# Twenty-nine of a graph kernel's gathers are replaced by row-by-row DMAs from ScalarE and SyncE

## The chip, the cores and the metric

One core of one Trainium2 chip. The core has five engines, each with its own in-order instruction stream: TensorE (PE; its weight loads are listed apart as PEld), VectorE (DVE), ScalarE (ACT), GpSimd (POOL) and SyncE (SP). They meet only at semaphores. DMAs are issued by ACT, SP and POOL and run beside the engines. The metric is device microseconds for one run of the kernel; less is better.

## The reference

One graph attention layer on 12,500 nodes of 128 features and 200,000 edges sorted by target node:

```python
edge_index = jnp.stack([src, dst])
h = jnp.maximum(_layernorm(x, axis=-1), 0.0)
x = x + _L0_gnn_ref(h, edge_index, edge_attr_64, W_node, W_edge, a)

# _L0_gnn_ref, 4 heads of 32 features:
h = (node_features @ W_node.T).reshape(num_nodes, H, HD)
e = (edge_features @ W_edge.T).reshape(num_edges, H, HD)
h_src = h[src]
h_tgt = h[tgt]
att = jnp.sum(jnp.concatenate([h_src, h_tgt, e], axis=-1) * a, axis=-1)
att = jnp.where(att > 0, att, 0.2 * att)
m = jnp.maximum(segment_max(att, tgt), 0.0)
ex = jnp.exp(att - m[tgt])
denom = segment_sum(ex, tgt) + (num_edges - deg)[:, None] * jnp.exp(-m)
w = ex / denom[tgt]
h_prime = segment_sum(w[:, :, None] * h_src, tgt)
```

So for each edge the row of its source node has to be fetched, weighed by a softmax over all edges of the same target, and added up at the target.

## The kernel before

A first part computes for every node one row of 137 floats (548 bytes): the 128 projected features with a one behind each head, a count, and the node's share of the attention for each head. The rows go to a table in DRAM (`table`), and all that follows works on edges.

The edges are cut into 392 groups of up to 511 (with one carried place, 512, stored as J = 4 chunks of 128). QG = 4 groups are a **quad** (98 quads), and up to four quads are a **superblock**; from quad 7 to 86 superblocks have four quads each, beginning at 7, 11, 15 and so on. Up to quad 35 a quad has one window of target nodes, up to 74 two, from 75 on four (`CLASSES`).

*Gathers.* `gather` (L171) has POOL issue one indirect DMA for each chunk (L183): it takes 128 places from `srci` and brings 128 rows into `ga`, one on each partition. `ga_all` is a ring of QUADS = 8 quads. `open_logits(q)` (L644) calls `fetch(q + 2)`, which issues quad q + 2's sixteen gathers. From quad 8 on, every gather adds to one semaphore for each ring place, and the reader waits for the sum.

*Logits.* `all_logits(q)` (L1368) runs ahead of the softmax: DVE compares targets (L656), PE multiplies edge features (L686) and adds the targets' share (L689), and ACT copies the result (`keep_logits`, tg, L699). `add_sources(q)` (L718) has ACT wait for all gathers of quad q and then copy the sources' attention out of `ga` into U (L733). It is called at the beginning of `all_logits(q + 1)`, behind that quad's first DVE comparison, or at the start of `softmax` for a superblock's last quad.

*Softmax.* `softmax(s)` (L769) works on a whole superblock once the U of its last quad is there: PE turns U (L790), ACT and DVE alternate (L795 to L872), PE turns the result back (L882), ACT copies it to xs (L888).

*Sums.* `sums(q)` (L1054) goes through the four groups of a quad, one **step** each: DVE weighs the gathered rows (L1041 or L1082) and builds the selection (L1024 or L1084), PE multiplies the two into the accumulator (L1115, four chunks, two records each), and in between `passed_on` (L934) has ACT compute an exponential (L943) and DVE pass a row on (L949). `complete(new)` ends a step, and `issue("inputs", "results")` follows. The sums of a superblock run beside the logits of the next.

*SP's queue.* SP issues, in the order written by `issue` (L592), results, input rows, edge features, targets and window weights (L596). For addresses that are known only at run time it first loads them from SBUF into registers (`windows`, L582; a TENSOR_LOAD in the trace).

The order of all this is written out by hand (`tc.manual_schedule()`): `together` runs the generators of logits, sums and softmax in turn, one yield each, and each engine executes its instructions in the order in which this emits them.

The targets' buffer `db_all` has room for two quads of 32-bit places. From quad OFFSETS = 10 on targets are bytes and use its first quarter only.

Of the kernel before, what the change touches and what calls it, by code (L numbers as in the profile page):

```python
# [9 lines left out]
F32 = mybir.dt.float32  # L10
# [4 lines left out]
OP = mybir.AluOpType  # L15
AX = mybir.AxisListType

P = 128
# [28 lines left out]
SQUARE = 32  # L47
TWO = 2
HELD = 3
SETS = max(NODE_T, QG * J)  # L50
PAD = 1 << 20

# [5 lines left out]
def class_of(q):  # L58

    return next(c[1:] for c in CLASSES if c[0] is None or q < c[0])  # L60
# [9 lines left out]
def kernel(  # L70
# [39 lines left out]
    nc = tc.nc  # L110
    NT = -(-(N + P) // P)
    NP = NT * P
# [8 lines left out]
    table = dram.tile([NP, ROW], F32, name="table")  # L121
# [33 lines left out]
    quads = blocks(G, QG)  # L155
    nq = len(quads)
# [7 lines left out]

    spare = consts.tile([P, 6 * SBG * H], F32, name="spare")
    ga_all = consts.tile([P, QUADS, QG, J, ROW], F32, name="ga")
    GA, GATHERED = {}, set()
    arrived = [tc.alloc_semaphore(f"rows{k}") for k in range(QUADS)]
    landings = {}

    def gather(q, rows, width, lo, hi):  # L171

        g0, m = quads[q]
        ga = GA[q] = ga_all[:, q % QUADS]
        chunks = lambda i: -(-min(E - (g0 + i) * NE + 1, GE) // P)
        for i in range(lo, hi):
            if chunks(i) < J:
                nc.vector.memset(ga[:, i, chunks(i):, :], 0.0)
        order = [(i, j) for i in range(lo, hi) for j in range(chunks(i))]
        if q >= 2 * QUADS:  # L180
            order.sort(key=lambda at: at != (hi - 1, 0))
        for i, j in order:
            came = nc.gpsimd.indirect_dma_start(  # L183
                out=ga[:, i, j, 0:width], out_offset=None, in_=rows,
                in_offset=bass.IndirectOffsetOnAxis(ap=srci[:, g0 + i, j:j + 1], axis=0))
# [16 lines left out]
    per = SBG // QG  # L202
# [15 lines left out]
    with tc.manual_schedule():  # L218
# [25 lines left out]
        for _ in range(AT_ONCE):  # L244
            q, i = early.pop(0)
# [129 lines left out]
        db_all = stay.tile([P, 2, QG, GE], I32, name="db")  # L375
# [20 lines left out]
        with tc.tile_pool(name="node", bufs=2) as node, tc.tile_pool(  # L396
# [6 lines left out]
            first = index.tile([1, W], F32, name="first")  # L403
# [110 lines left out]
            for b, (t0, T) in enumerate(sets):  # L514
# [5 lines left out]
                row = node.tile([P, NODE_T, ROW], F32, name="row")  # L520
# [24 lines left out]
    with tc.tile_pool(name="work", bufs=2) as work, \  # L545
# [34 lines left out]
        def windows(of, size, w, n):  # L580
# [52 lines left out]
        def fetch_rows(s):  # L633
            g0, m = groups(s)
            dr = DR[s] = turned.tile([SBG * H, NE + 2], I32, name="dr", bufs=2)
            if finer(s) > 1:
# [4 lines left out]
            nc.sync.dma_start(dr[0:H * m, :],  # L641
                              dst_rows[g0:g0 + m, :].unsqueeze(0).to_broadcast([H, m, NE + 2]))

        def open_logits(q):  # L644
            if q == supers[of_quad[q]][0]:
                fetch_rows(of_quad[q])
            if q + 2 < nq:
                fetch(q + 2)
            AT[q] = work.tile([P, QG, GE], BF16, name="at")
# [68 lines left out]
        def add_sources(q):  # L718

            s = of_quad[q]  # L720
            g0, m = quads[q]
            s0, sm = groups(s)
            keep_logits(q)
            if s not in U:
                U[s] = turned.tile([P, J, SBG * H], F32, name="U", bufs=2)
            f = finer(s)
            u = U[s][:, 0:J // f, 0:sm * H * f].rearrange("p c (h w) -> p w c h", h=H)[
                :, (g0 - s0) * f:(g0 - s0 + m) * f]
            if q >= QUADS:
# [3 lines left out]
            taken = nc.scalar.copy(u, GA[q][:, :m].rearrange("p g (f c) r -> p (g f) c r", f=f)[  # L733
                :, :, :, R_SRC:R_SRC + H])
# [160 lines left out]
        state = {"step": 0}  # L895

        def complete(window=True, all_due=False):

            state["step"] += 1
            division = None  # L900
            if divisions and "hold" not in state and (
                    all_due or divisions[0][-1] is None or divisions[0][-1] + 2 <= state["step"]):
                division = divisions.pop(0)
            if begun and window:
                complete_window(*begun.pop())
            if division:
                divide(*division)
# [146 lines left out]
        def sums(q):  # L1054
# [7 lines left out]
            g0, m = quads[q]  # L1062
            s = of_quad[q]
# [3 lines left out]
            k, span = class_of(q)  # L1067
# [23 lines left out]
            for i in range(m):  # L1091
                g = g0 + i
                if first_fold - 4 <= q < first_fold - 4 + FOLDS:
                    shifts(q + 4, i)
                on_gpsimd = early and (q, i) > (first_fold - 2, QG - 2)
                if (q, i) not in AHEAD:
                    weighed(nc.gpsimd if on_gpsimd else nc.vector, ga, i,
                            heads(XE[s] if on_gpsimd else ex)[:, :, :, g - s0])
                    if not early:
                        mark(q, i, hot)  # L1100
                new = i % k == 0
                if not i and not later:
                    entered()
                    settled()
                if new:
                    second = k == 2 and i > 0
                    if not second:
                        bank = ps.tile([P, 512], F32, name="acc", bufs=3)
                    acc = bank[0:1 + span, ROW:2 * ROW] if second else bank[0:1 + span, 0:ROW]
                    fc = fac if g == s0 else None  # L1110
                if later and i == m - 1:
                    entered()
                least_j = 1 if k == 1 else 0
                for j in range(least_j, J)[::-1]:
                    nc.tensor.matmul(acc, hot[:, i, j, 0:1 + span], ga[:, i, j, :],  # L1115
                                     start=new and j == J - 1 and not second,
                                     stop=k > 1 and i % k == k - 1 and j == least_j,
                                     skip_group_check=k > 1)
                if i == (2 if later else 1):
                    passed_on(fac if g0 == s0 else None)  # L1120
                    if later:
                        settled()
                if not later and i == (2 if k > 1 else 1):
                    entered()
                    if k == 1:
                        settled()
                complete(new)
                if k == 1:
                    begun.append((q, i, ga, hot, pt, acc, fc))
                if i == 2 and QUADS <= q < first_fold - 5 and of_quad[q + 1] == s:  # L1130
# [715 lines left out]
```

## Time and profile before

| | before |
|---|---|
| median of 3 runs | 1998.38 us (1997.35 to 1998.41) |
| the profiled execution: time, span | 1998.91 us, 1997.1 us |
| POOL busy | 1496.7 us (75%), 1596 instructions |
| DVE busy | 1195.0 us (60%) |
| PE busy | 1130.1 us (57%), mean granted clock 0.734 |
| ACT busy | 318.9 us (16%) |
| gathers from `table` (L183) | 1494, 946 ns mean |

A line of the groups reads: line, engine, operation, out<-in, shapes, count; then busy time and the mean of one in ns; then the engine's idle time just before them and what ended most of it. A line of the timeline reads: start and duration in us, engine, line, operation, out<-in, shapes, count; in brackets the engine's idle time before it and what ended it. SPq and ACTq are the sequencers of SP and ACT: DMA issues and register loads, which are not counted as busy. A line of one source line's view reads: line, engine, operation, count; durations min/median/max in ns; first and last start in us.

### The profile page before, as it was taken

To read this page: it belongs to the slowest core of one execution; us is meant where nothing else is said; L and a number is where in the kernel's file an instruction comes from. 1 tells how busy PE (TensorE), PEld (TensorE's weight loads), DVE (VectorE), ACT (ScalarE), POOL (GpSimd) and SP (SyncE) were. 2 spreads that over 40 slices of the span, in tenths; PEclk is the share of its full clock that TensorE was granted. 3 is DMA by queue.
4 is the path that set the end of the run, shared out by engine and by line. 5 is a ranking of instruction groups with operands and counts; after the bars stand their busy time and mean duration, and the time that the engine had idled before them with its cause. 6 is when DMAs were issued, how large, how long until landed. Compare 5 with 4: busy or idle time off the path is not lost.

```text
span 1997.1 us, 18760 instructions
## 1 busy us (share of the span) xinstructions
PE 1130.1 (57%) x5116; PEld 771.6 (39%) x5116; DVE 1195.0 (60%) x2666; ACT 318.9 (16%) x1077; POOL 1496.7 (75%) x1596
## 2 busy tenths in 40 slices
PE   6566675555464645554646455546464555365555
PEld 4444454334243333343434333434343333243344
DVE  8676886456374554563755546637555475376675
ACT  6564111001001010010010100101101011121222
POOL 7777777777777777777777777777777777777775
PEclk9788788676676776766767767667677677677777
DMA  7753754434344434344444444444443453444441
GB/s 253 208 138 95 179 131 114 99 98 109 98 110 102 119 98 106 104 109 111 113 105 121 98 112 107 110 111 112 107 117 94 106 123 97 110 108 115 106 102 43
DMA packets 167747, 229.56 MB, mean 115 GB/s; under 512 B 60827, under 2 KB 100669, under 8 KB 167638
## 3 DMA queue, kind: packets, MB, share of 16 engines
q0 software_dynamic: 50112, 109.61, 24.5%
q1 hardware_dynamic: 115824, 116.14, 20.1%
q10 hardware_dynamic: 1702, 2.59, 0.4%
q8 instruction: 41, 0.67, 0.1%
q14 instruction: 68, 0.56, 0.1%
HBM read 210.74 MB, written 17.43 MB: 114 GB/s over the span
## 4 chain that ended last, share of the span: by engine, by line
POOL 41%; DVE 24%; issue 16%; PE 7%; DMA 6%; ACT 5%; SPq 0%; ACTq 0%; POOLq 0%; DVEq 0%
POOL ga L183 41%; DMA ga<-table,srci 5%; DVE at L656 3%; PE t_ps L790 2%; DVE ga L1041 1%; DVE t_ps L865 1%; DVE t_ps L804 1%; DVE t_ps L803 1%; DVE t_ps L862 1%; PE ex_ps L882 1%; DVE hot L1024 1%; PE acc L1115 1%; DVE stats L287 1%; ACT ga L309 1%; DVE pt L949 1%
## 5 line engine op out<-in xcount | busy, mean ns | idle before, releaser
L183 POOL DMA_INDIRECT ga<-table,srci x1494 | 1413.4, 946 | 456.7 <-issue 429.4
L1115 PE MATMUL acc<-ga,hot 128*113 128x137 f32 (+1 forms) x2928 | 539.4, 343 | 77.7 <-DVE hot L1024 53.3
L1115 PEld LDWEIGHTS acc<-ga,hot 128*113 128x113 f32 (+1 forms) x2928 | 479.9, 213 | 176.6 <-issue 94.5
L949 DVE SCALAR_TENSOR_TENSOR pt<-pt,spare,acc 1x133 f32<-1x133 f32 x113 | 38.2, 338 | 522.0 <-ACT den_of L943 520.6
L689 PE MATMUL lg<-at,pw 112*96 112x512 bf16 (+2 forms) x392 | 155.5, 433 | 278.1 <-DVE at L656 265.4
L686 PE MATMUL lg<-ea,by_pair 128*96 128x512 f32 (+1 forms) x392 | 227.8, 666 | 6.4 <-ACT tg L699 6.4
L656 DVE TENSOR_TENSOR at<-const_ps,db 112x1024 bf16<-112x1024 f32 (+1 forms) x176 | 212.9, 1210 | 4.5 <-DMA db<-offset 4.5
L1082 DVE TENSOR_TENSOR ga<-ga,ex_ps 128x1056 f32<-128x1056 f32 x147 | 182.2, 1240 | 0.0
L790 PE MATMUL t_ps<-ident,U 128*64 128x128 f32 (+2 forms) x210 | 46.8, 395 | 217.5 <-ACT U L733 217.5
L733 ACT COPY U<-ga 128x64 f32<-128x64 f32 x98 | 29.0, 297 | 815.8 <-DMA ga<-table,srci 815.8
L1084 DVE TENSOR_TENSOR hot<-const_ps,slot 128x896 f32<-128x896 f32 (+1 forms) x147 | 144.2, 981 | 0.0
L790 PEld LDWEIGHTS t_ps<-ident,U 128*64 128x64 f32 (+2 forms) x210 | 36.8, 200 | 243.8 <-ACT U L733 240.1
L882 PE MATMUL ex_ps<-ident,stack 128*128 128x128 f32 x105 | 28.6, 424 | 178.2 <-DVE stack L872 166.9
L968 PEld LDWEIGHTS acc<-pt,spare 1*2 1x2 f32 x226 | 14.0, 86 | 208.8 <-issue 199.9
L689 PEld LDWEIGHTS <-pw 112*96 112x96 bf16 (+2 forms) x392 | 53.9, 137 | 100.9 <-issue 98.4
L882 PEld LDWEIGHTS ex_ps<-ident,stack 128*128 128x128 f32 x105 | 18.5, 214 | 192.1 <-ACT stack L870 192.1
L183 POOL DMA_INDIRECT ga<-in_x_dram,srci x72 | 68.6, 952 | 23.2 <-issue 19.2
L1041 DVE TENSOR_TENSOR ga<-ga,ex_ps 128x528 f32<-128x528 f32 x92 | 63.6, 693 | 36.6 <-ACT xs L888 36.5
L699 ACT COPY tg<-lg 96x512 f32<-96x512 f32 (+1 forms) x51 | 29.5, 579 | 294.0 <-PE lg L689 294.0
L913 PE MATMUL acc<-ga,hot 128*81 128x137 f32 x176 | 42.6, 330 | 54.9 <-ACT ga L921 52.9
L715 PE MATMUL t_ps<-tg,of_head 96*64 96x512 f32 (+3 forms) x96 | 71.6, 838 | 0.0
L715 PEld LDWEIGHTS t_ps<-tg,of_head 96*64 96x64 f32 (+3 forms) x96 | 11.9, 172 | 153.8 <-issue 151.6
(204 smaller groups left out, 1324.9 us busy)
## 6 DMA issues: line engine op xcount, KB each, us to landing
ea<-in_edge_t_dram SPq DMA_DIRECT2D x196, 256.0 KB
ga<-table,srci POOLq DMA_INDIRECT x1494, 2.6
db<-offset SPq DMA_DIRECT2D x53, 256.0 KB
db<-in_dst_dram SPq DMA_DIRECT2D x20, 320.0 KB
db<-offset SPq DMA_DIRECT2D x35, 160.0 KB
table<-row SPq DMA_DIRECT2D x9, 616.5 KB
xt<-in_x_dram SPq DMA_DIRECT2D x9, 576.0 KB
inputs<-in_x_dram SPq DMA_DIRECT2D x92, 56.0 KB
```

The costliest lines, as they stand in the source:

```text
L183: came = nc.gpsimd.indirect_dma_start(out=ga[:, i, j, 0:width], out_offset=None, in_=rows, in_offset=bass.IndirectOffsetOnAxis(ap=srci[:, ...
L656: nc.vector.tensor_tensor(AT[q][:span, i:i + n, :].rearrange("p g e -> p (g e)"), part_ps[:span].to_broadcast([span, n * GE]), DB[q][:span ...
L686: nc.tensor.matmul(lg, by_pair[:, begin:begin + n], ea[:, i // 2, :], start=half == 0 and i == 0, stop=False, skip_group_check=True)
L689: nc.tensor.matmul(lg, PW[q][:span, begin:begin + n], at[:span, i, :], start=False, stop=full and i == quads[q][1] - 1, skip_group_check=True)
L715: nc.tensor.matmul(TP[s][:groups(s)[1] * H], of_head[supers[s][1], p][:n], tg[:n], start=p == 0, stop=False, skip_group_check=True)
L790: nc.tensor.matmul(t_ps[:R, j * P:(j + 1) * P], u[:, j, :R], ident, start=False, stop=j == C - 1, skip_group_check=True)
L882: nc.tensor.transpose(turned_ps[:, j, :], stack[:, j * P:(j + 1) * P], ident)
L949: nc.vector.scalar_tensor_tensor(to, row(w + at), passing[:, w + at:w + at + 1], own, op0=OP.mult, op1=OP.add)
L1041: engine.tensor_tensor(val, val, weight.unsqueeze(3).to_broadcast([P, J, H, HW]), op=OP.mult)
L1082: nc.vector.tensor_tensor(val, val, weight.unsqueeze(3).to_broadcast([P, TWO * J, H, HW]), op=OP.mult)
L1084: nc.vector.tensor_tensor(hot[:, i:i + TWO, :, 1:1 + span].rearrange("p g j c -> p (g j) c"), lane_ps[:, 0:span].unsqueeze(1).to_broadcast ...
L1115: nc.tensor.matmul(acc, hot[:, i, j, 0:1 + span], ga[:, i, j, :], start=new and j == J - 1 and not second, stop=k > 1 and i % k == k - 1 a ...
```

## The change

29 of the chunks, the fourth or third chunk of the last group of some quad, are no longer gathered by POOL. Each is brought as 128 DMAs of one row (548 bytes, one partition) each:

- **ACT's 16 chunks** (fourth chunk, j = 3), for quads 16, 20, 24 ... 76: one for each superblock of four quads that begins at quad 11, 15 ... 71, for the second quad of the next superblock. In `add_sources` of the superblock's four quads, ahead of the wait for gathers, ACT issues 12, 30, 54 and 32 of the rows (`IN_WAITS`).
- **SP's 13 chunks** (third chunk, j = 2), for quads 20, 24, 29 ... 77: from quad 10 on SP issues seven rows behind each step of the sums, so a chunk takes 19 steps.

The place of a row comes from `src`: a small DMA brings a chunk's 128 places into one partition, DVE multiplies them by the row's size in bytes, and the issuing engine loads them into registers, up to 27 (ACT) or 21 (SP) at a time. Rows and places lie in the part of `db_all` that targets no longer use, two buffers for each engine. A semaphore counts a chunk's rows; ACT waits for it in `add_sources` of the quad the chunk belongs to and copies the 128 rows into `ga`.

```diff
+SINGLES_FROM = 10
+IN_WAITS = 12, 30, 54, 32
+LOADED = 27
...
-        order = [(i, j) for i in range(lo, hi) for j in range(chunks(i))]
+        order = [(i, j) for i in range(lo, hi) for j in range(chunks(i)) if (q, i, j) not in SINGLE]
...
+        class Singles:
+            def __init__(self, engine, kind, some, j, at):
...
+                free = db_all.rearrange("p k g e -> p k (g e)")[:, :, GE * (1 + at):GE * (2 + at)]
+                self.rows = [free[:, k, 0:ROW].bitcast(F32) for k in range(2)]
+                self.places = [free[0:1, k, 2 * P:3 * P] for k in range(2)]
+                self.semaphores = [nc.alloc_semaphore(f"single{at}_{k}") for k in range(3)]
...
+            def fetch_places(self, n):
+                if n < len(self.of):
+                    g = quads[self.of[n]][0] + QG - 1
+                    at = ((g // 2 * J + self.j) * 2 + g % 2) * P
+                    self.engine.dma_start(self.places[n % 2], src[at:at + P].unsqueeze(0))
+
+            def scale_places(self, n):
+                if n < len(self.of):
+                    nc.vector.tensor_scalar(self.places[n % 2], self.places[n % 2], float(4 * ROW),
+                                            None, op0=OP.mult)
+
+            def advance(self):
+                n, at = divmod(self.step, self.steps)
+                self.step += 1
+                if n < len(self.of):
+                    self.some_rows(n, at * self.some, min(at * self.some + self.some, P))
+
+            def in_wait(self, q):
+                q0, m = supers[of_quad[q]]
+                if q0 + m + 1 in self.of:
+                    k = q - q0
+                    self.some_rows(self.of.index(q0 + m + 1), sum(IN_WAITS[:k]), sum(IN_WAITS[:k + 1]))
+
+            def some_rows(self, n, lo, hi):
+                if not lo:
+                    assert self.of[n] not in GATHERED
+                    SINGLE[self.of[n], QG - 1, self.j] = self, n
+                    if not n:
+                        self.fetch_places(0)
+                        self.scale_places(0)
+                    self.fetch_places(n + 1)
+                    self.loaded = 0
+                if lo < P // 2 <= hi:
+                    self.scale_places(n + 1)
+                for p in range(lo, hi):
+                    if p >= self.loaded:
+                        upto = min(p + (LOADED // self.some * self.some if self.some else
+                                        min(LOADED, hi - p)), P)
+                        self.values = p, nc.values_load_multi_w_load_instructions(
+                            self.places[n % 2][:, p:upto], engines=[self.kind], min_val=0,
+                            max_val=(NP - 1) * 4 * ROW,
+                            skip_runtime_bounds_check_because="a node's row")[1]
+                        self.loaded = upto
+                    came = self.engine.dma_start(
+                        as_bytes(self.rows[n % 2][p:p + 1, :]),
+                        rows_at(table, self.values[1][p - self.values[0]], 4 * ROW, 1))
+                    came.then_inc(self.semaphores[n % 3], 16)
...
+            def put(self, n, to):
+                assert self.count[n] == P
+                nc.scalar.wait_ge(self.semaphores[n % 3], 16 * P * (n // 3 + 1))
+                taken = nc.scalar.copy(to, self.rows[n % 2])
...
+        SINGLES = [Singles(*of, at) for at, of in enumerate([(nc.scalar, mybir.EngineType.Activation, None, 3), (nc.sync, mybir.EngineType.SP, 7, 2)])]
...
         def add_sources(q):
...
+            for of in SINGLES:
+                if not of.some:
+                    of.in_wait(q)
+            for (a, i, j), (of, n) in list(SINGLE.items()):
+                if a == q:
+                    of.put(n, GA[q][:, i, j, :])
+                    del SINGLE[a, i, j]
             if q >= QUADS:
                 nc.scalar.wait_ge(arrived[q % len(arrived)],
...
                 complete(new)
+                if q >= SINGLES_FROM:
+                    for of in SINGLES:
+                        if of.some:
+                            of.advance()
```

More of the change, by code (lines that the diff above doesn't have):

```diff
@@ L166 @@
     ga_all = consts.tile([P, QUADS, QG, J, ROW], F32, name="ga")
-    GA, GATHERED = {}, set()
+    GA, GATHERED, SINGLE = {}, set(), {}
     arrived = [tc.alloc_semaphore(f"rows{k}") for k in range(QUADS)]
@@ L642, in fetch_rows @@
                               dst_rows[g0:g0 + m, :].unsqueeze(0).to_broadcast([H, m, NE + 2]))
+        class Singles:
+            def __init__(self, engine, kind, some, j, at):
+                self.engine, self.kind, self.some, self.j = engine, kind, some, j
+                free = db_all.rearrange("p k g e -> p k (g e)")[:, :, GE * (1 + at):GE * (2 + at)]
+                self.rows = [free[:, k, 0:ROW].bitcast(F32) for k in range(2)]
+                self.places = [free[0:1, k, 2 * P:3 * P] for k in range(2)]
+                self.semaphores = [nc.alloc_semaphore(f"single{at}_{k}") for k in range(3)]
+                self.step, self.count, self.used = 0, {}, 0
+                if some:
+                    self.steps = -(-P // some)
+                    last = QG * sum(class_of(q)[0] > 1 for q in range(SINGLES_FROM, nq)) // self.steps
+                    first = SINGLES_FROM + 5 + -(-self.steps // QG)
+                    self.of = [first + n * self.steps // QG for n in range(last)]
+                else:
+                    self.of = [q0 + m + 1 for q0, m in supers
+                               if m == per and q0 >= SINGLES_FROM and class_of(q0 + m - 1)[0] > 1]
+            def fetch_places(self, n):
[41 more added lines that the diff above has]
+                    came.then_inc(self.semaphores[n % 3], 16)
+                    tc.no_tile_sem_insts.add(came.ins.name)
+                    tc.add_to_no_dep_group(f"single{self.j}_{n}", came.ins)
+                    self.count[n] = self.count.get(n, 0) + 1
+            def put(self, n, to):
+                assert self.count[n] == P
+                nc.scalar.wait_ge(self.semaphores[n % 3], 16 * P * (n // 3 + 1))
+                taken = nc.scalar.copy(to, self.rows[n % 2])
+                tc.declare_no_dep(taken.ins, group=f"single{self.j}_{n}",
+                                  reason="a semaphore counts the rows of this chunk")
+                tc.declare_fence(taken.ins, group=f"single{self.j}_{n}")
@@ L644, in open_logits @@
+        SINGLES = [Singles(*of, at) for at, of in enumerate([(nc.scalar, mybir.EngineType.Activation, None, 3), (nc.sync, mybir.EngineType.SP, 7, 2)])]
         def open_logits(q):
+            state["opened"] = q
             if q == supers[of_quad[q]][0]:
```

## The prediction

> **What bounds the kernel now.** I read the page first, then GpSimd's (POOL's) timeline from first gather to last, and then the timelines of the engines that use what is gathered. The page:
>
> ```profile
> span 1997.1 us, 18760 instructions
> PE 1130.1 (57%) x5116; PEld 771.6 (39%) x5116; DVE 1195.0 (60%) x2666; ACT 318.9 (16%) x1077; POOL 1496.7 (75%) x1596
> ...
> L183 POOL DMA_INDIRECT ga<-table,srci x1494 | 1413.4, 946 | 456.7 <-issue 429.4
> ```
>
> The first and last gather in POOL's timeline:
>
> ```profile
> 3.14 1.16 POOL L183 DMA_INDIRECT ga<-in_x_dram,srci  x1 [1.60 <-DMA srci<-in_src_by_edge_dram]
> ...
> 1962.48 0.94 POOL L183 DMA_INDIRECT ga<-table,srci  x1 [0.30 <-issue]
> ```
>
> POOL is only 75% busy, but its idle time is 0.30 us in front of each gather that nothing explains: 1494 gathers from the table and 72 from x, 1566 in all, stand back to back from 3.14 to 1963.4, which is 1.25 us each. So the gathers set the end, and 34 us of tail follow the last one. POOL is the present bound; a gather less is 1.25 us less, for as long as POOL stays the bound.
>
> Next, ScalarE (ACT) over one superblock, quads 43 to 46, and into the next. Every quad has one L733 copy, so its place in that line's order is its quad: 906.17 is quad 44, 966.04 is quad 47.
>
> ```profile
> 906.17 0.30 ACT L733 COPY U<-ga 128x64 f32<-128x64 f32 x1 [9.09 <-DMA ga<-table,srci]
> ...
> 926.17 0.30 ACT L733 COPY U<-ga 128x64 f32<-128x64 f32 x1 [19.35 <-DMA ga<-table,srci]
> ...
> 934.04 0.58 ACT L699 COPY tg<-lg 96x512 f32<-96x512 f32 x1 [7.23 <-PE lg L689]
> 946.09 0.30 ACT L733 COPY U<-ga 128x64 f32<-128x64 f32 x1 [11.47 <-DMA ga<-table,srci]
> ...
> 964.42 0.37 ACT L888 COPY xs<-ex_ps 128x256 f32<-128x256 f32 x1 [1.32 <-PE ex_ps L882]
> ...
> 966.04 0.31 ACT L733 COPY U<-ga 128x64 f32<-128x64 f32 x1 [0.89 <-DMA ga<-table,srci]
> 966.20 0.17 ACT L943 ACTIVATE den_of<-acc 113x8 f32<-113x8 f32 x1
> ...
> 976.35 0.58 ACT L699 COPY tg<-lg 96x512 f32<-96x512 f32 x1 [9.17 <-PE lg L689]
> ```
>
> Over a superblock of 80 us ACT waits for gathers 9.09 + 19.35 + 11.47 + 0.89 = 40.8 us. The other 39 us are not free: they are waits for work that ACT's own copy started (7.9 us from the copy of quad 45 to the tg copy at 934.04, 18.3 us from quad 46's to the xs copy, 10.3 us from quad 47's to the next tg). VectorE (DVE) shows that it hangs on ACT there:
>
> ```profile
> 926.53 0.72 DVE L949 SCALAR_TENSOR_TENSOR pt<-pt,spare,acc 1x133 f32<-1x133 f32 x2 [11.26 <-ACT den_of L943]
> ...
> 970.42 0.70 DVE L949 SCALAR_TENSOR_TENSOR pt<-pt,spare,acc 1x133 f32<-1x133 f32 x2
> ```
>
> L943 is queued on ACT right behind the L733 copy. In the quad of 926 DVE stands 11.26 us for it, so each us by which ACT comes late there is a us for the whole consumer side. At a superblock's first quad (970.42) DVE has other work until 970.42 and does not wait: L943 stood at 966.2, so some 4.1 us of lateness are hidden there.
>
> For the stage that the change touches, quads 11 to 74, the waits of ACT from 268 to 1506 us:
>
> ```profile
> ACT U L733 <- DMA ga<-table,srci: 638.3, 61, 19.4
> ACT tg L699 <- PE lg L689: 246.0, 32, 11.8
> ```
>
> **638.3 us** over 16 superblocks is all the room that ACT has without being late.
>
> **What the change removes.** 29 gathers at 1.25 us are 36.2 us of POOL's stream. If POOL stays the bound, the time is 1998.9 - 36.2 = 1962.7. (The profiled execution took 1998.91 us, 1.8 more than its span, and the median of the runs is 1998.38; half a us apart, so sums on the one hold for the other.)
>
> **What it adds on ACT.** 16 of the chunks go to ACT, one a superblock: 16 x 128 = 2048 rows. Each row costs ACT's sequencer a DMA issue, a register's handling, and its share of the load that brings the row's place from SBUF into a register. All three stand in ACT's order ahead of its wait and its copy. The nearest rows for the issue are ACT's one DMA onto a single partition in this stage, and SyncE's (SP's) with an address from a register:
>
> ```profile
> L1466 ACTq DMA_DIRECT2D rows<-in_dst_ends_dram x1: 245/245/245, 427.0 to 427.0; - x1
> ```
>
> ```profile
> 933.98 0.32 SPq L596 DMA_DIRECT2D pw<-side  x1
> 934.35 0.42 SPq L596 DMA_DIRECT2D ea<-in_edge_t_dram  x1
> 934.81 0.43 SPq L596 DMA_DIRECT2D db<-offset  x1
> 935.37 0.35 SPq L596 DMA_DIRECT2D pw<-side  x1
> ```
>
> One partition costs 0.245 us. Between issues lie 0.04 to 0.05 us where the address is fixed (ea at 934.35, db at 934.81) and 0.13 where it comes from a register (db ends at 935.24, pw begins at 935.37); I take 0.11, nearer to the second since each row has a register. Issue and handling: 0.355 us. For the load, the same line in three stages, where a load brings one, two and four places:
>
> ```profile
> L582 SPq TENSOR_LOAD <-base_row x20: 262/268/308, 281.7 to 631.9; - x20
> ```
>
> ```profile
> L582 SPq TENSOR_LOAD <-base_row x31: 467/476/517, 812.6 to 1410.2; - x31
> ```
>
> ```profile
> L582 SPq TENSOR_LOAD <-base_row x9: 868/878/1037, 1692.2 to 1833.9; - x9
> ```
>
> 0.268, 0.476 and 0.878 us: 0.20 us for each place and 0.07 for the load, a straight line, so that 27 places in one load are 5.5 us and save little over single loads. A row is therefore **0.555 us** of ACT. The bounds: from below 0.495 (gap 0.05), from above 0.66 (the 0.32 of a many-partition issue, gap 0.13, place 0.21). That no load of 27 stands in the trace leaves a case where places come cheaper in bulk; it is a rival below.
>
> The Trainium skill, "Runtime: NRT & Kernel Launch", section "Instruction fetch mechanics", says that loading a register takes about 200 ns even in bulk. That speaks against this change; the trace agrees up to four places (0.20 us each), and by the rule a load of 27 would be an estimated 5.4 us, the sum staying as it is.
>
> ACT's sum: 2048 x 0.555 = 1136.6 us. Seven loads a superblock (12; 27 and 3; 27 and 27; 27 and 5) by 0.07 by 16: 7.8. The 29 copies of a landed chunk (128x137) are dearer than the L733 copy of 128x64 (0.30) and cheaper than the L699 copy of 96x512 (0.58): I take 0.35, 10.2 in all. 16 DMAs for the places, 0.29 each: 4.6. Together **1159 us against 638.3 us of room**. Of the excess, 16 x 4.1 = 65.6 hide behind DVE at first quads, and I let 15 hide in the first superblock, where quads 11 to 13 show no wait for a gather (61 of 64 copies wait) and DVE and PE set the pace (an estimate; between 0 and 25). The consumers fall behind by 1159.2 - 638.3 - 65.6 - 15 = **440 us** by quad 74, 27 us a superblock.
>
> **What the lateness does to POOL.** A gather of quad q writes the ring place of quad q - 8 and must wait for its last reading by PE. Counted by L1115's records, 32 a quad, quad 44's end with this group:
>
> ```profile
> 993.20 2.17 PE L1115 MATMUL acc<-ga,hot 128*113 128x137 f32 x8
> ```
>
> That is 995.4. Quad 52's first gather (the 761st from the table: quad 4 has its last eight from there, and each later one sixteen) starts at
>
> ```profile
> 1044.62 0.95 POOL L183 DMA_INDIRECT ga<-table,srci  x1 [0.30 <-issue]
> ```
>
> which is 49.2 us later. So 49.2 us of lateness cost nothing, and the rest stops POOL for as long: 440 - 49 = 391. From quad 82 on POOL runs freely again, the consumers catch up there, and the end moves by 391: **1998.9 + 391 = 2390 us**. POOL's 36 us are lost in its new waits. With the bounds of a row: 0.495 gives 2048 x 0.495 + 22.6 - 718.9 = 317, end 2267; 0.66 gives 655, end 2605.
>
> **SP.** Seven rows behind a step are 28 a quad. The first half of its present work in one quad:
>
> ```profile
> 951.31 0.35 SPq L596 DMA_DIRECT2D out_dram<-res  x1
> 951.71 0.43 SPq L596 DMA_DIRECT2D ea<-in_edge_t_dram  x1
> 952.95 0.34 SPq L596 DMA_DIRECT2D out_dram<-res  x1
> 953.91 1.28 SPq L596 DMA_DIRECT2D inputs<-in_x_dram  x2
> ```
>
> These, and four as at 933.98 to 935.37 above, are with the loads and the gaps some 5.4 us; 28 x 0.555 and the loads' 0.1 make 15.6 more: 21.0 us a quad, of the 26.8 that a quad then takes. Behind SP's rows are queued results, inputs of the next quad and features two quads ahead; each is late by up to 3.9 us, less than it is ahead. I cost SP at nothing; without ACT's lateness as cover it would be 1 us a quad over 62 quads (13 chunks by 19 steps by a quarter), 62 us less the ring's 49. DVE's 29 scalings of one row of places, each shorter than the 0.70 us of L949's pair, fall into its waits for L943. A chunk's last rows are issued more than a quad ahead of the copy that waits for them; gathers land so:
>
> ```profile
> DMA to landing us min/median/max: 2.5/3.0/7.9
> ```
>
> Even 7.9 us is less than a quad.
>
> **The rivals.**
> 1. *Faster: a row is cheap.* If a load of 27 costs what a load of one does, a row is 0.245 + 0.05 + 0.01 = 0.305 us; ACT's sum is 647 us, under its room with the hidden part (719), and POOL's 36.2 us come out in full: **1963**. For it: the rows are cut by waits (54 ahead of a 19.35 us wait), and ACT is 16% busy. Against it: the straight line of the loads. It decides below 0.364 us a row, where consumers are 49 us late.
> 2. *No change:* at 0.365 the lateness (51) eats the ring's room while POOL is 36 ahead: 1962.7 + 51 + 36 - 49 = **2001**, and within a few us of before on either side.
> 3. *Slower, but part hides:* the rows also fill ACT's 246.0 us of waits for PE's logits. Then 440 - 246 - 49 = 145: **2144**. Against it: those waits begin only after the late copy has gone.
> 4. *Dearer still:* if 54 issues in a row fill a DMA queue and each takes 0.43 us (the db row above) with the same gap and place, a row is 0.74: 2048 x 0.74 + 22.6 - 718.9 - 49.2 = 770, **2769**. The trace has no such burst.
>
> **How the numbers follow.** My forecast (2267 to 2605) 0.60; part hides (2040 to 2267) 0.13; dearer (over 2605) 0.08; no change 0.03; faster 0.16. About 0.2% is what a measurement of this kernel can tell from no change. So slower 0.81, same 0.03, faster 0.16. The range leaves out the faster case, the unchanged one and the far end of the dearer: 2040 to 2680.
>
> **What would show it.** Right: POOL with waits for PE's L1115 in place of 0.30 us gaps, from the second superblock on, some 390 us in all; no wait of L733 for gathers between quads 15 and 74, but ACT's sequencer with rows 0.5 to 0.6 us apart; DVE's wait for L943 longer by 5 to 10 us a quad; loads of 27 places at 5.4 us; superblocks of about 107 us. Wrong: rows under 0.36 us apart and gathers still 1.25 us apart, 1537 of them; or DVE's waits for L943 unchanged while ACT is full of rows, which would mean that the consumers do not hang on ACT as I read it.

## The result, and the profile after

The changed kernel takes 2262.07 us (median of 4, 2260.28 to 2263.79), the kernel before beside it 1998.39 (4 runs, 1997.35 to 1998.95): a ratio of 1.1322, 95% interval 1.1304 to 1.134. It is 264 us slower. I had predicted 2390, with 2267 as the end of its own lower bound. Three of the kernels below were first timed together on a chip that no other experiment used, where the kernel before itself took 2469.82 us instead of 1998; times of that slower group are not set against the others, and two of the three kernels were run again.

The page of the changed kernel: span, the engines, and the group of the gathers from the table.

```profile
span 2260.7 us, 26497 instructions
...
PE 1145.3 (51%) x5116; PEld 777.2 (34%) x5116; DVE 1200.2 (53%) x2695; ACT 326.5 (14%) x1106; POOL 1469.1 (65%) x1567
...
L186 POOL DMA_INDIRECT ga<-table,srci x1465 | 1386.1, 946 | 747.9 <-issue 730.9
```

Busy times say nothing of the loss: POOL does 28 us less, and each other engine at most 15.2 us more. The instructions are 7737 more, nearly all on the sequencers, and they aren't counted as busy. What grew is POOL's idle time in front of the gathers. POOL's waits before (total, times, longest) and after:

```profile
POOL ga L183 <- issue: 448.6, 1472, 0.3
```

```profile
POOL ga L186 <- issue: 749.8, 1474, 11.6
```

301 us more, nearly all of it in 51 stops of 1.1 to 11.6 us among the steady 0.30. The first, of 3.1 us, ends at 366.72 us, late in the stage's first superblock; these two lines stand around the first one above 4 us, in the second superblock:

```profile
423.56 0.94 POOL L186 DMA_INDIRECT ga<-table,srci  x1 [0.31 <-issue]
435.58 0.94 POOL L186 DMA_INDIRECT ga<-table,srci  x1 [11.08 <-issue]
```

The profile names no releaser ("issue"), but the times do. That gather is the first of quad 21, and the ring place that it writes was last read by PE's sums of quad 13, whose last records end at 434.81, 0.77 us before it:

```profile
433.24 1.57 PE L1209 MATMUL acc<-ga,hot 128*81 128x137 f32 x6
```

So it is in all 51: each stands ahead of the first gather of a quad, and that gather starts 0.76 to 0.77 us after PE's last record for the quad eight before (L1209's records counted, 32 a quad).

ACT's timeline over one superblock, from quad 45's copy (1102.04) to quad 49's (1200.73), shows who is late. ACTq are its sequencer's records, x54 the number of rows issued:

```profile
1102.04 0.30 ACT L827 COPY U<-ga 128x64 f32<-128x64 f32 x1 [30.00 <-issue]
...
1112.32 12.44 ACTq L711 DMA_DIRECT2D db<-table  x32
1124.81 0.30 ACT L827 COPY U<-ga 128x64 f32<-128x64 f32 x1 [14.37 <-issue]
...
1145.12 4.13 ACTq L711 DMA_DIRECT2D db<-table  x12
1149.29 0.30 ACT L827 COPY U<-ga 128x64 f32<-128x64 f32 x1 [5.39 <-DVE hot L1178]
...
1158.37 11.24 ACTq L711 DMA_DIRECT2D db<-table  x30
1169.65 0.51 ACT L723 COPY ga<-db 128x137 f32<-128x137 f32 x2 [13.47 <-issue]
...
1176.29 24.40 ACTq L711 DMA_DIRECT2D db<-table  x54
1200.73 0.30 ACT L827 COPY U<-ga 128x64 f32<-128x64 f32 x1 [29.90 <-issue]
```

Each copy comes as soon as the rows ahead of it have been issued; none waits for a gather. The superblock takes 98.7 us instead of 80. ACT's and DVE's waits in the stage, 282 to 1840 us:

```profile
ACT U L827 <- issue: 620.1, 28, 30.5
ACT ga L723 <- issue: 301.7, 20, 29.9
ACT tg L786 <- PE lg L776: 171.9, 30, 7.3
```

```profile
DVE pt L1043 <- ACT den_of L1037: 791.8, 61, 23.0
```

ACT's 638.3 us of waits for gathers in this stage are gone altogether; "issue" in front of its copies stands there instead. DVE's wait for ACT was, in the stage of before (268 to 1506 us):

```profile
DVE pt L949 <- ACT den_of L943: 475.2, 46, 15.2
```

### The profile page after: what moved, and what is told of

Same layout as the page of the kernel before. It is cut to its first block, busy times and chain, and to the rows that moved or that the text cites. A ratio compares the mean times of both kernels' runs of the same rounds, so it can differ in the third digit from the quotient of the medians.

```text
span 2260.7 us, 26497 instructions
## 1 busy us (share of the span) xinstructions
PE 1145.3 (51%) x5116; PEld 777.2 (34%) x5116; DVE 1200.2 (53%) x2695; ACT 326.5 (14%) x1106; POOL 1469.1 (65%) x1567
## 5 line engine op out<-in xcount | busy, mean ns | idle before, releaser
L186 POOL DMA_INDIRECT ga<-table,srci x1465 | 1386.1, 946 | 747.9 <-issue 730.9
L1209 PE MATMUL acc<-ga,hot 128*113 128x137 f32 (+1 forms) x2928 | 545.5, 346 | 77.3 <-DVE hot L1118 48.5
L1209 PEld LDWEIGHTS acc<-ga,hot 128*113 128x113 f32 (+1 forms) x2928 | 486.1, 215 | 178.6 <-issue 90.8
L773 PE MATMUL lg<-ea,by_pair 128*96 128x512 f32 (+1 forms) x392 | 236.1, 688 | 6.7 <-ACT tg L786 6.7
L773 PEld LDWEIGHTS lg<-ea,by_pair 128*96 128x96 f32 (+1 forms) x392 | 64.6, 190 | 12.9 <-ACT tg L786 8.3
```

The costliest lines, as they stand in the source:

```text
L186: came = nc.gpsimd.indirect_dma_start(out=ga[:, i, j, 0:width], out_offset=None, in_=rows, in_offset=bass.IndirectOffsetOnAxis(ap=srci[:, ...
L773: nc.tensor.matmul(lg, by_pair[:, begin:begin + n], ea[:, i // 2, :], start=half == 0 and i == 0, stop=False, skip_group_check=True)
```

## The experiments

### Which of the two engines' rows: one at a time, and neither

In the first two kernels one entry of the list is left and the other engine's chunks go back to POOL.

```diff
 act_alone
-SINGLES = [... (nc.scalar, ..., None, 3), (nc.sync, ..., 7, 2)]
+SINGLES = [Singles(nc.scalar, mybir.EngineType.Activation, None, 3, 0)]
 sp_alone
+SINGLES = [Singles(nc.sync, mybir.EngineType.SP, 7, 2, 1)]
 left_out: some_rows and put without their bodies (29 chunks stay out of GA)
```

> ACT's 16 chunks alone; SP's 13 go back to POOL's gathers. Theory (ACT's sequencer, filled with rows ahead of its waits, sets the pace of the consumers; SP's rows cost nothing): a superblock stays at 98 us, and the time at 2250 to 2265 us; POOL stands for as long as in the changed kernel. Rival (the two streams of rows together hold each other or the gathers back, or SP's rows make results and features late): without SP's rows the time falls to 2000 to 2150 us.

> SP's 13 chunks alone; ACT's 16 go back to POOL's gathers. Theory: SP needs some 18.5 us of a quad's 20 with loads of 21 places, so its rows hide; POOL has 13 gathers less and stays back to back: 1998.4 - 13 x 1.25 = 1982 us. Rival (SP's rows make results, inputs or features late): over 2000 us, and if SP is the whole cause of the slowdown, up to 2260.

> The 29 chunks are neither gathered nor brought as rows (those 29 x 128 edges read what the ring place held before, so the sums over them are not the reference's). Theory (POOL is the bound of the kernel before, back to back): 1998.4 - 29 x 1.25 = 1962 us, POOL still without gaps. Rival (another chain ends nearly as late as POOL): 1980 to 1998 us.

| kernel | median us | ratio to before, 95% |
|---|---|---|
| act_alone | 2254.2 | 1.1289 (1.1267 to 1.1312) |
| sp_alone | 1981.56 | 0.9921 (0.9905 to 0.9938) |
| left_out | 1961.69 | 0.9822 (0.9806 to 0.9839) |

POOL's waits, of act_alone, sp_alone and left_out:

```profile
POOL ga L186 <- issue: 731.9, 1488, 11.1
```

```profile
POOL ga L186 <- issue: 443.4, 1454, 0.3
```

```profile
POOL ga L186 <- issue: 439.4, 1440, 0.7
```

All three came out as the theory had them. With 29 gathers less and nothing in their place the kernel is 35.3 us faster than before in the same group (1997.02), 1.22 us a gather: POOL is the bound before. SP's 1664 rows cost nothing and POOL keeps its 0.3 us gaps; its 13 gathers come out almost whole (15.5 us of 16.3). ACT's rows alone make nearly the whole loss, 257 of 264 us.

### Rows or places: loads of one place

Each load brings a single place, and all rows of that load use it; the number of loads, rows and gathers stays.

```diff
-                            self.places[n % 2][:, p:upto], engines=[self.kind], ...
+                            self.places[n % 2][:, p:p + 1], engines=[self.kind], ...
...
-                        rows_at(table, self.values[1][p - self.values[0]], 4 * ROW, 1))
+                        rows_at(table, self.values[1][0], 4 * ROW, 1))
```

> As the changed kernel, but each load brings one place only, and all rows of that load's part are fetched from this one place (so the 29 chunks hold wrong rows, and the sums over them are not the reference's); the row DMAs keep their register and their number. It takes away the loads' places and leaves the issues. Theory (the excess over ACT's room is mostly loads): ACT's loads fall from 20.1 to about 3.5 us a superblock, the consumers' lateness at quad 74 from 311 to 45 us, which fits into the ring's room but for the 36 us that POOL is ahead: 1985 to 2005 us, superblocks of 82 us or less. Rival (2048 issues alone, 0.325 us each, are too many): above 2100 us.

The profiled execution took 2000.02 us (before in that group: 1999.97). A second execution, of which there is no profile, took 3770.12 us; why stays open, so this reading rests on one execution. ACT's timeline from quad 48 to 49:

```profile
1021.50 18.81 ACTq L711 DMA_DIRECT2D db<-table  x54
1040.36 0.30 ACT L827 COPY U<-ga 128x64 f32<-128x64 f32 x1 [18.81 <-issue]
```

The 54 rows take 18.81 us instead of 24.40 with their places loaded. With the issues alone ACT just uses up its room and the ring's: by quad 74 the consumers are 50 us late (below). This is the second rival of the prediction (a row of 0.365 us gives 2001) made real: a row here is 0.344 us (below) and its part of seven loads of some 0.55 us 0.03, 0.374 in all. On top of issues that already fill the room, it is the loads of places that turn no change into 264 us.

### The start of a load: aligned, and moved by one value

In the changed kernel loads of one size take very different times. The seven loads of the superblock shown above, each alone in its stretch of the line's view (median of one record, start). They are in order of time 27 places from place 96, 5 from 123, 12 from 0, 27 from 12, 3 from 39, 27 from 42, 27 from 69:

```profile
L706 ACTq TENSOR_LOAD <-db x1: 2325/2325/2325, 1109.9 to 1109.9; - x1
...
L706 ACTq TENSOR_LOAD <-db x1: 1393/1393/1393, 1121.5 to 1121.5; - x1
...
L706 ACTq TENSOR_LOAD <-db x1: 1067/1067/1067, 1143.9 to 1143.9; - x1
...
L706 ACTq TENSOR_LOAD <-db x1: 2353/2353/2353, 1155.6 to 1155.6; - x1
...
L706 ACTq TENSOR_LOAD <-db x1: 980/980/980, 1167.4 to 1167.4; - x1
...
L706 ACTq TENSOR_LOAD <-db x1: 5956/5956/5956, 1170.2 to 1170.2; - x1
...
L706 ACTq TENSOR_LOAD <-db x1: 6088/6088/6088, 1185.2 to 1185.2; - x1
```

27 places cost 2.3 us from place 96 or 12, and 6.0 from 42 or 69. 96 and 12 are multiples of four (16 bytes, counted from the start of the buffer, whose own address no view shows), 42 and 69 are not. The rival is that the part of the buffer or the order of the loads decides. One kernel cuts the parts so that every load starts on a multiple of four; another leaves all as it is and moves the buffer by one value.

```diff
 aligned
-IN_WAITS = 12, 30, 54, 32
-LOADED = 27
+IN_WAITS = 12, 28, 56, 32
+LOADED = 28
 shifted, shifted_2
-                self.places = [free[0:1, k, 2 * P:3 * P] for k in range(2)]
+                self.places = [free[0:1, k, 2 * P + 1:3 * P + 1] for k in range(2)]
```

> ACT takes 12, 28, 56 and 32 rows instead of 12, 30, 54 and 32, and loads of up to 28 places instead of 27, so every load of both engines begins at a multiple of 16 bytes (SP: 28, four steps' worth, instead of 21). In the changed kernel loads that begin at such a place take 2.33 us for 27 places, others 5.96 to 6.09. Theory (the address decides): loads of 28 take 2.4 us, ACT saves some 8 us a superblock, 2262 - 16 x 8 = 2134 us (2110 to 2160). Rival (a load is slow where rows or copies run just before it): loads stay at 6 us in the third part, 2250 to 2270 us.

> The changed kernel with one edit: the buffer of a chunk's 128 places begins one value (4 bytes) further on. Number and sizes of the loads, rows, issues, waits and gathers stay as they are. If the start's place in 16 bytes decides what a load costs, ACT's loads at 0, 12 and 96 now start off a multiple of four and go from 1.07, 2.33 and 2.32 us to some 2.5, 5.6 and 5.6, those at 39 and 123 come to start on one and fall from 0.98 and 1.39 to some 0.5 and 0.6, and those at 42 and 69 stay near 6: 6.7 us a superblock more, 107 over 16 superblocks, and 2262 + 107 = 2369 us (2350 to 2375). If it is the size of the load, or which part of the buffer it reads, that made some loads cheap: 2262 us, and the loads as they were.

> The same kernel as shifted (the places begin 4 bytes further on), run again for its time. Its loads in the first run were, by superblock, 2.87, 5.91, 0.98, 6.05, 4.90, 5.98 and 0.82 us, 27.5 together against 20.1 with the places where they were: 7.4 more, 118 over 16 superblocks. If the consumers pay each us of ACT's order, as they did for the 10.8 us a superblock that alignment saved, this kernel takes 2262 + 118 = 2380 us (2365 to 2390).

The loads of aligned (28 places in most, 4 in the shortest):

```profile
L706 ACTq TENSOR_LOAD <-db x96: 580/1904/2087, 282.2 to 1638.8; - x96
```

The loads of shifted_2 that answer to 27 from 96, 12 from 0, 27 from 12 and 3 from 39 of the changed kernel:

```profile
L706 ACTq TENSOR_LOAD <-db x1: 5951/5951/5951, 1297.4 to 1297.4; - x1
...
L706 ACTq TENSOR_LOAD <-db x1: 2903/2903/2903, 1334.3 to 1334.3; - x1
L706 ACTq TENSOR_LOAD <-db x1: 5956/5956/5956, 1349.4 to 1349.4; - x1
L706 ACTq TENSOR_LOAD <-db x1: 995/995/995, 1364.5 to 1364.5; - x1
```

aligned takes 2088.51 us (ratio 1.0459, 1.0439 to 1.048): 174 us faster than the changed kernel by 10.8 us a superblock of loads (9.4 against 20.2, all of a kernel's loads over 16). shifted_2 takes 2406.32 (1.205, 1.2028 to 1.2071): 144 us slower by 8.5 us a superblock (28.7 against 20.2). So the start decides, and the consumers pay each us of ACT's order. My expectations missed by size: aligned was expected at 2134 (places are cheaper than I took them), shifted_2 at 2380 (its load of 27 places from 70 took 6.1 us, not the 4.9 of the first run). In the slower group shifted took 3245.8 us; its loads were lengthened in the same way (the load of 12 from 1.07 to 2.87 us, 27 from 12 to 5.91), but the load of 27 from 70 took anything from 3.1 to 6.0 us there, which the start does not explain.

In the runs on the other chips ACT's loads lie within 0.4 us, nine in ten within 0.15, of 0.36 us + 0.207 us for each unit, where a unit is four places as long as the load starts on a multiple of four, and one place otherwise or for the rest: 28 aligned are 7 units (1.81 by this, 1.90 measured), 27 aligned 6 + 3 (2.22; 2.33), 27 others 27 (5.95; 5.96), 3 from place 40 three (0.98; 0.995). That is a fit, not a look into the chip.

### Fewer chunks on ACT

Can ACT recover in a superblock without rows? One kernel leaves every other chunk of ACT's to POOL, one takes aligned loads, three superblocks of four, and eight rows a step on SP.

```diff
 every_other
-                               if m == per and ... and class_of(q0 + m - 1)[0] > 1]
+                               if m == per and ... and class_of(q0 + m - 1)[0] > 1][1::2]
 three_of_four: aligned, SP 8 rows a step, and
+                    self.of = [q for k, q in enumerate(self.of) if k % 4]
```

> ACT takes a chunk in every other superblock only (8 chunks, the second, fourth and so on), in 12, 30, 54 and 32 rows with loads of 27 as in the changed kernel; SP's 13 stay. Theory (what counts is ACT's excess beyond the room of waits, and the ring of eight quads lends 49 us): each loaded superblock is some 18 us late, the next makes it good out of its 40 us of waits, POOL never stands: 1998.4 - 21 x 1.25 = 1972 us (1968 to 1978). Rival (each late copy of ACT costs its time whenever it happens): 8 x 18 = 144 us more, 2110 us or so.

> Loads that begin at multiples of 16 bytes (12, 28, 56, 32 rows, loads of 28), ACT's chunks in three of four superblocks (12, not in the first), SP with eight rows a step (16 chunks, loads of 24): 28 gathers less. Theory: a loaded superblock is 8 us late against before and POOL is 6 us ahead by fewer gathers, so the consumers fall 14 us behind POOL in each, 42 in three, under the ring's 49, and come back in the fourth; SP needs about 18 of a quad's 19 us: 1998.4 - 28 x 1.25 = 1963 us (1960 to 1970). Rival (the ring's room is used up before the fourth, or SP's eight rows make features or results late): 1975 to 2000 us.

every_other takes 1985.97 us (0.9928, 0.9912 to 0.9945), three_of_four 1976.36 (0.9883, 0.9866 to 0.9899). Both are faster than before, and both miss by 13 to 14 us. ACT's copies of quads 45, 49, 53, 57 and 61 in every_other:

```profile
914.38 0.30 ACT L827 COPY U<-ga 128x64 f32<-128x64 f32 x1 [3.34 <-DMA ga<-table,srci]
...
1021.88 0.30 ACT L827 COPY U<-ga 128x64 f32<-128x64 f32 x1 [29.70 <-issue]
...
1076.99 0.30 ACT L827 COPY U<-ga 128x64 f32<-128x64 f32 x1
...
1189.64 0.30 ACT L827 COPY U<-ga 128x64 f32<-128x64 f32 x1 [30.15 <-issue]
...
1244.85 0.30 ACT L827 COPY U<-ga 128x64 f32<-128x64 f32 x1
```

From quad 45 to 53 are 162.6 us, from 53 to 61 another 167.9, while POOL, which took 80 us a superblock before and has one chunk of ACT's and some 1.7 of SP's fewer in two, needs 160 - 2.7 x 1.25 = 156.6. From quad 49 to 53 (and 57 to 61) ACT has only the last 32 of a chunk's rows to issue, and the consumers take 55 us without a wait for a gather. Half of POOL's 156.6 is 78, so they make good 23 us there, less than the 29 that they lose from quad 45 to 49 (107.5 us). So lateness piles up, and my expectation, which had every other superblock recover in full, was wrong.

The next kernel puts the two together: every other superblock, aligned loads, eight rows a step on SP, 24 gathers fewer. With it, SP's eight rows by themselves.

```diff
 half_and_eight, half_and_eight_2: aligned, [1::2] as above, and
-... (nc.sync, mybir.EngineType.SP, 7, 2)])]
+... (nc.sync, mybir.EngineType.SP, 8, 2)])]
 sp_eight: aligned, and
+SINGLES = [Singles(nc.sync, mybir.EngineType.SP, 8, 2, 1)]
```

> ACT takes its chunk in every other superblock (8 chunks), every load starts on a multiple of four places (parts of 12, 28, 56, 32; at most 28 a load), SP issues eight rows a step (16 chunks): 24 gathers fewer. A loaded superblock should take 88.5 us as in the kernel with aligned loads, an unloaded one what the consumers need by themselves. With 21 gathers fewer and unaligned loads a pair of superblocks took 163 to 168 us against 160 before, its loaded half 108 or 98, so lateness piled up until the ring's 49 us were gone late in the stage. If that is the cause, 10 to 20 us less in the loaded half bring a pair under POOL's pace of some 156 to 160, the ring is not used up, and all gathers come out: 1998.4 - 24 x 1.25 = 1968 us (1966 to 1972). If something else held those kernels 13 us short (the rows of SP, or the copies of landed chunks), about 1980.

> SyncE's rows alone, eight a step instead of seven (16 chunks, 16 gathers fewer), its loads of 24 places all starting on a multiple of four. ACT brings no rows. If SP's rows hide as they did with seven a step: 1998.4 - 16 x 1.25 = 1978 us (1976 to 1980). If at eight a step SP becomes late with inputs or results: over 1983 us.

> The same kernel as half_and_eight (ACT's chunk in every other superblock, aligned loads, SP eight rows a step, 24 gathers fewer), run again, since in the group of that run the kernel before itself took 2470 us instead of 1998. The expectation is unchanged: 1968 us (1966 to 1972) if a loaded and an unloaded superblock together stay under POOL's pace; about 1980 if something else held the two kernels before it 13 us short.

half_and_eight_2 takes 1968.32 us (1967.85 to 1968.77), ratio 0.9859 (0.9841 to 0.9877): what was expected, and the fastest kernel here with the whole computation. ACT's copies of quads 45, 49 and 53, and POOL's waits:

```profile
913.05 0.30 ACT L827 COPY U<-ga 128x64 f32<-128x64 f32 x1 [18.23 <-DMA ga<-table,srci]
...
999.88 0.30 ACT L827 COPY U<-ga 128x64 f32<-128x64 f32 x1 [22.50 <-issue]
...
1069.52 0.30 ACT L827 COPY U<-ga 128x64 f32<-128x64 f32 x1 [15.93 <-DMA ga<-table,srci]
```

```profile
POOL ga L186 <- issue: 444.6, 1456, 0.8
```

The pair takes 156.5 us, at both of its ends ACT waits for a gather again, and POOL has no stop above 0.8 us in the stage.

The first runs of half_and_eight (2903.16 us) and sp_eight (2818.76, ratio 1.1419) were of the slower group, as was shifted; there rows of SP took up to 1398 ns against 308 ns in sp_alone (L711's view):

```profile
L711 SPq DMA_DIRECT2D db<-table x2048: 1/228/1398, 430.3 to 2330.0; - x187
```

```profile
L711 SPq DMA_DIRECT2D db<-table x1664: 224/228/308, 306.0 to 1522.1; - x185
```

Why, stays open, and with it what sp_eight by itself takes beside a kernel before of 1998 us. That eight rows a step hide beside ACT's rows, half_and_eight_2 shows.

## Why the prediction was right

**The bound before** was POOL's stream of gathers: left_out. **SP at nothing**: sp_alone, though the rows do fill it. SP's wait for DVE's results, its largest before, then in sp_alone and in the changed kernel:

```profile
SPq L596 <- DVE res L1328: 883.1, 72, 16.5
```

```profile
SPq L599 <- DVE res L1426: 100.3, 19, 16.7
```

```profile
SPq L599 <- DVE res L1426: 404.4, 62, 22.1
```

In sp_alone some 780 us of it are used and 100 left; the 404 of the changed kernel are there because ACT's lateness stretches every quad.

**The path**, rows in ACT's order ahead of its copy, DVE and PE late by as much, POOL stopped by the ring (the 0.77 us above), is what the traces show, and act_alone shows that nothing else is needed. Of the signs: no wait of ACT for gathers in the stage; POOL's stops from the second superblock on (one of 3.1 us before), 301 us in all (predicted some 390); DVE's wait for L1037 up by 316.6 us over 62 quads, 5.1 each (predicted 5 to 10). One sign was told wrongly: the profile puts POOL's stops down to "issue", and only the times of PE's records tie them to its sums.

**The ring's 49.2 us** was the firmest number. The copies of quad 74 (the 75th of their line), before, after, in aligned, shifted_2 and one_place:

```profile
1505.35 0.30 ACT L733 COPY U<-ga 128x64 f32<-128x64 f32 x1 [11.50 <-DMA ga<-table,srci]
```

```profile
1816.50 0.30 ACT L827 COPY U<-ga 128x64 f32<-128x64 f32 x1 [14.32 <-issue]
```

```profile
1641.04 0.30 ACT L827 COPY U<-ga 128x64 f32<-128x64 f32 x1 [13.09 <-issue]
```

```profile
1963.06 0.30 ACT L827 COPY U<-ga 128x64 f32<-128x64 f32 x1 [17.47 <-issue]
```

```profile
1555.42 0.30 ACT L827 COPY U<-ga 128x64 f32<-128x64 f32 x1 [11.70 <-issue]
```

Late is the difference to 1505.35, the end moved is the profiled span less 1997.1. If the ring lends 47.6 us (taken from the first row) and removed gathers are worth 1.25 us each, the end moves by the larger of "late less 47.6" and "gathers taken out":

| kernel | quad 74 late | late - 47.6 | gathers out | end moved |
|---|---|---|---|---|
| after | 311.2 | 263.6 | -36 | 263.6 |
| shifted_2 | 457.7 | 410.1 | -36 | 410.2 |
| aligned | 135.7 | 88.1 | -36 | 87.9 |
| one_place | 50.1 | 2.5 | -36 | 1.1 |
| every_other | 39.2 | -8.4 | -26 | -9.8 |
| three_of_four | 27.3 | -20.3 | -35 | -23.1 |
| half_and_eight_2 | -16.8 | -64.4 | -30 | -30.1 |

(Quad 74's copy starts at 1544.57, 1532.66 and 1488.53 us in the last three. act_alone, sp_alone and left_out fit within 1 us: the end moved by 258.7, -17.1 and -36.4 for 259.3, -16.2 and -36.2.) This also tells where the 13 us of every_other and three_of_four went: consumers that are 39 or 27 us late still hold POOL, because POOL itself wants to be 26 or 35 us ahead, and both take from the same 47.6.

**The size was off by 128 us**, 2390 against 2262, and at 2262 the time lies 5 us below the range of my own forecast (2267 to 2605), in the one that I had given to "part hides" with a chance of 0.13. The mechanism came out as forecast; that the time still lies in the range of 2040 to 2680 is luck, owed to the room left for another mechanism. The terms that were mis-sized are ACT's:

| term | predicted | measured |
|---|---|---|
| a row's issue and register | 0.355 us, 727 for 2048 rows | 0.344 us, 704 |
| places, with the loads' own 0.07 | 0.20 us each, 417 in all | 20.2 us a superblock, 323 |
| copies of landed chunks, DMAs for places | 15 us | not measured apart; 15 kept |
| ACT's sum | 1159 us | 1042 us |
| hidden of the excess over 638.3 | 81 us | 93 us (1042 - 638.3 - 311) |
| a superblock | 107 us | 98.7 us |
| consumers late by quad 74 | 440 us | 311 us |

The row's 0.344 is the mean distance of the starts of two rows with no load between them (1936 of them on ACT; the median is 0.325). The rows shown of the timeline give the same: 54 rows in 24.40 us with a load of 6.09 among them are (24.40 - 6.09 - 0.23) / 53 = 0.341. So the issues were sized well; eight tenths of what ACT's sum was too large by (94 of the sum's 117 us) are the places. A row with its places cost 0.344 + 323 / 2048 = 0.50 us, just above the lower bound of 0.495, and the time is just under that bound's 2267. The measured sum put into the prediction's own formula (1042 - 718.9 - 49.2) gives 274 us, 10 more than the 263.6 by which the end moved: the hidden part was 93 us, not 81.

The step that failed in kind, not only in size, is "0.20 us for each place and 0.07 for the load, a straight line, so that 27 places in one load are 5.5 us". It holds for loads that start off a 16-byte boundary (5.96 and 6.09 us) and not for the others (2.33). Three sizes from one line fitted a line, but which places these loads started from I did not ask. By the kernel's count of windows (one a quad up to 35, two up to 74, then four) the loads of four begin at window 114, 118 and so on, two past a multiple of four; loads of one and two have as many units by the fit wherever they start. So none of the three sizes could show a cheaper load. The line was also SP's: one place costs SP 0.268 us, but ACT 0.55 (the median in one_place). The Trainium skill, "Runtime: NRT & Kernel Launch", section "Instruction fetch mechanics", has loading a register at about 200 ns even in bulk (for register loads that the runtime injects; here the kernel loads from SBUF); the runs agree off the boundary (5.96 / 27 = 0.22 us) and disagree on it (1.90 / 28 = 0.068 us), and here the measurement decides.

**The rivals.** "Faster, a row is cheap" was wrong for this kernel, but its break-even of 0.364 us a row, and the "no change" beside it, were right: one_place, at 0.374 us, came out even. "Part hides" in ACT's 246.0 us of waits for PE's logits gave 2144; those waits shrank to 171.9 us in the stage, 74 less, without the rows standing in them: rows come behind the logits' copy in ACT's order. Summed by copy, whatever ended the wait, ACT's idle time there shrank only behind the superblocks' first quads (138.2 us before, 73.8 after, 16 waits each; behind the third quads 107.8 and 106.5): about the 65.6 us which the sum already counts as hidden. "Dearer" had the 54 rows at 0.43 us each; in the bursts here the median issue took 0.235 us and the longest 0.615 (min/median/max in ns):

```profile
L711 ACTq DMA_DIRECT2D db<-table x2048: 227/235/615, 283.0 to 1816.2; - x187
```

There is no sign of a queue that fills. In the slower group it was otherwise: there shifted's rows came 0.63 us apart in the mean and up to 2.8. What held them is open, so "dearer" is refuted for the other runs only.

## What to carry to other kernels

Before work is put "into the waits" of an engine that issues in order, add up what its sequencer will do there, issues and register loads too, against the waits it has in a period. What doesn't fit is paid by everyone behind it, once the buffers' slack is gone; and slack that a producer's lead has used is not there for a consumer's lateness. A price that is read from small cases should be asked what else those cases have in common: here it was the address.

## What the runs showed of the hardware that I had not expected

- A load of several registers from SBUF costs less where it starts on a multiple of 16 bytes from its buffer's start: 28 places 1.90 us, 27 places 2.33, against 5.96 for 27 that start elsewhere. To move one buffer by 4 bytes made the kernel 144 us slower, to cut its loads on that boundary 174 us faster.
- A burst of single-row issues on ACT runs at 0.34 us a row over 54 rows, as over 12 (4.13 us, 0.35 a row), in all runs but those of the slower group.
